# Attention's values made in four column tiles and turned by VectorE, with a fixed order for the attention's entrance and end

## The chip, the cores and the metric

One core of one Trainium2 chip runs the whole program. The metric is the device time of one execution in microseconds (us); lower is better. TensorE (PE in the profile) multiplies matrices and writes into PSUM; ScalarE (ACT) and VectorE (DVE) take the results from there; GpSimd (POOL) does sums in SBUF and issues some transfers, SyncE (SP) issues the others.

## The reference

Sixteen images of 256 channels, 28 x 28 pixels, pass four layers: a convolution with binary weights (layer 0), a block of binary convolutions with gates (layer 1), two binary convolutions with batch normalisation and a residual (layer 2), and an attention over the 784 pixels of each image (layer 3). Only the last is touched:

```python
def _L3_conv_ref(x, Wq, Wk, Wv, Wp):       # x: 16 x 256 x 28 x 28, float32
    C_RED = 64
    xf = x.reshape(B, C, N)                            # N = 784
    q = jnp.einsum('rc,bcn->bnr', Wq, xf)
    k = jnp.einsum('rc,bcn->brn', Wk, xf)
    v = jnp.einsum('rc,bcn->bnr', Wv, xf)
    attn = jnp.einsum('bnr,brm->bnm', q, k) * (1.0 / sqrt(64))
    attn = jax.nn.softmax(attn, axis=-1)
    out = jnp.einsum('bnm,bmr->brn', attn, v)
    out = jnp.einsum('cr,brn->bcn', Wp, out)
    return out.reshape(B, C, H, W) + x
```

The end of layer 2 is done at the start of the attention, image by image: `prelu(y * scale + shift + x, a3)`.

## The kernel before

An image lies in SBUF as x[b], 128 partitions x 2 channel halves x 784 pixels. The attention works on it transposed: the scores are laid out with 112 keys on the partitions (7 chunks of keys, c) and the 784 queries in two halves (h) of 392 along the free axis. The exponential is taken without subtracting a maximum; `watch` looks for overflow, and a second program part (not entered here) would redo the attention if it found one. Each image has these steps, and the loop weaves three images together:

- finish_a, finish_b, finish_c: the end of layer 2 for image b + 3 or b + 2 (normalise, relu, combine). From image 3 on the residual is added by a transfer that accumulates (`p<-x2d`); finish_c also stores the image for the second part (`xd`).
- queries_keys and project_v: queries, keys and values of the next image. PSUM tile `mi` holds queries on partitions 0 to 63 and keys on 64 to 127. The pool `ps_mi` has one buffer, and the projection at the end of an image uses it too.
- scores, exponentials `es`, sums of them for the softmax's denominator, values: 7 chunks each.
- denominators, reciprocal, normalisation, projection with Wp and the sum with x, store.

All operands are float32, for which the hardware does each matmul of the source in two passes; the profile counts both. `manual_schedule` keeps the instructions of each engine in the order of the source; outside of it the order is chosen by a scheduler. In the profile, L1084 is finish_a, L1094 finish_b (`rl`), L1099 finish_c, L1112 the queries' and keys' matmul (`mi`), L1116, L1118 and L1119 its copies, L1127 the scores (`sc`), L1131 the exponential, L1148 values (`av`) and denominators (`sm`), L1188 and L1192 the values' matmul and copy (`va`), L1198 the projection. x[b] is named `p` there.

```python
    pssc = ctx.enter_context(tc.tile_pool(name="ps_sc", bufs=2, space=PSUM))
    psav = ctx.enter_context(tc.tile_pool(name="ps_av", bufs=1, space=PSUM))
    psmi = ctx.enter_context(tc.tile_pool(name="ps_mi", bufs=1, space=PSUM))
    pssm = ctx.enter_context(tc.tile_pool(name="ps_sm", bufs=1, space=PSUM))
    ones = ph.tile([MC, 64], F32, name="ones64")
    nc.gpsimd.memset(ones, 1.0)
    # ... (na3, one_bank; two_banks gives a tile of two PSUM banks)

    def finish_a(b, n=slice(0, N)):
        for k in range(2):
            v = x[b][:, k, n]
            A.activation(v, v, AF.Identity, bias=bg3[:, k:k + 1], scale=sg3[:, k:k + 1])
            if b < 3:
                V.tensor_tensor(v, v, x2[b][:, k, n], ALU.add)
        if b >= 3:
            nc.gpsimd.dma_start(out=x[b], in_=x2d[b], accum_op=ALU.add)

    def finish_b(b, n=slice(0, N)):
        for k in range(2):
            if n.start == 0:
                rls[k] = buf(f"rl{k}", 1, shape=(P, N))
            A.activation(rls[k][:, n], x[b][:, k, n], AF.Relu, scale=-1.0)

    def finish_c(b, n=slice(0, N)):
        for k in range(2):
            v = x[b][:, k, n]
            V.scalar_tensor_tensor(v, rls[k][:, n], na3[:, k:k + 1], v, ALU.mult, ALU.add)
        if n.stop == N:
            nc.sync.dma_start(out=xd[b], in_=x[b])

    def queries_keys(b):
        ps = two_banks(psmi, "mi")
        q, k_ = qs[b], ks[b] = buf("q", 2, shape=(P, HN)), buf("k", 2)
        for h in range(2):
            for k in range(2):
                T.matmul(
                    ps[:, h, :HN], lhsT=wqk[:, k, :], rhs=x[b][:, k, h * HN:(h + 1) * HN],
                    start=(k == 0), stop=(k == 1),
                )
        A.copy(k_[64:P], ps[64:P, :, :HN])
        for h in range(2):
            A.copy(q[64 * h:64 * h + 64], ps[0:64, h, :HN])
        V.tensor_copy(k_[0:64], ps[64:P, :, :HN])

    # ... scores(b, c): for h in range(2) a matmul of 64 rows, lhsT = 112 keys of k_, rhs = q,
    # into the two banks of "sc"; then A.activation(es, sc, AF.Exp, scale=0.125)
    # ... sum_up: sums of es, chunks 0 to 3 on GpSimd, 4 to 6 on VectorE; sum_all adds the two
    # side_by_side: two matmuls, h = 0 and 1, into partitions 0 to 63 and 64 to 127
    # ... values: side_by_side(avs[b], va[b % 2][:, c, 0:64], es[b, c], ...) into PSUM "av"
    # take_values: ScalarE copies av to o; denominators: side_by_side(dns[b], ones, sums, ...)
    # invert: V.reciprocal(r, dns); normalize: V.tensor_tensor(o, o, r, mult)
    # watch: two ScalarE passes over dns and r with accum_out, which look for overflow

    def project_v(b):
        ps = one_bank(pssm, "sm")
        for c in range(NC_):
            for k in range(2):
                T.matmul(
                    ps[:MC, c * 64:(c + 1) * 64], lhsT=x[b][:, k, c * MC:(c + 1) * MC], rhs=wv[:, k, :],
                    start=(k == 0), stop=(k == 1),
                )
        A.copy(va[b % 2][:, :, 0:64], ps[:MC, :NC_ * 64].rearrange("p (c r) -> p c r", r=64))

    # ... project(b, mo): two matmuls, lhsT = wp, rhs = o, into a tile "mi" of psmi (or the one
    # given); then V.tensor_tensor adds it to x[b][:, mo]
    # ... store: nc.sync.dma_start(out=out[b], in_=x[b])

    for b in range(3):
        load_x2(b)
    for h in range(2):
        for step in (finish_a, finish_b, finish_c):
            step(0, slice(h * HN, h * HN + HN))
    queries_keys(0)
    scores(0, 0)
    project_v(0)
    for step in (finish_a, finish_b, finish_c):
        step(1)
    finish_a(2)

    with tc.manual_schedule(engines={ET.PE, ET.Activation, ET.DVE, ET.Pool}):
        for b in range(B):
            last = b == B - 1
            scores(b, 1)
            if b > 0:
                take_values(b - 1)
            if b > 1:
                project(b - 2, 0)
            sum_up(b, 1)
            scores(b, 2)
            if b > 0:
                sum_up(b - 1, 6)
            scores(b, 3)
            sum_up(b, 2, 3)
            if b > 1:
                watch(b - 2)
            finish_b(b + 2)                  # if b + 2 < B, as finish_c
            queries_keys(b + 1)              # if not last, as project_v
            project_v(b + 1)
            sum_all(b - 1)
            finish_c(b + 2)
            scores(b, 4)
            scores(b, 5)
            if b > 1:
                project(b - 2, 1)
                store(b - 2)
            sum_up(b, 5)
            if b + 3 < B:
                finish_a(b + 3)
            for c in range(4):
                values(b, c)
            if b > 0 and not last:
                denominators(b - 1)
                invert(b - 1)
            scores(b, 6)
            # ... (if not last:)
            scores(b + 1, 0)
            for c in range(4, NC_):
                values(b, c)
            normalize(b - 1)
            # ... (if last: denominators, reciprocal, projection and store of b - 1 among these)
        b = B - 1
        denominators(b)
        pss = [two_banks(pssc, "sc") for mo in range(2)]
        # ... in two parts n of 196 queries: take_values for both; then for each invert,
        # normalize, watch, project(b, mo, pss[mo], n) for mo = 0, 1; then store(b, mo) for both
```

Ahead of the attention 45 unused matmuls (`keep_busy`) hold TensorE active while the last statistics of layer 2 are worked out.

## Time and profile before

| | |
|---|---|
| time, median of 3 runs | 1153.67 us (1153.47 to 1154.21) |
| span of the profiled execution | 1151.9 us |
| mean granted TensorE clock | 0.991 |
| TensorE busy (matmul) | 1113.7 us, 97% |
| TensorE weight loads | 948.5 us, 82% |
| VectorE busy | 801.2 us, 70% |
| ScalarE busy | 711.5 us, 62% |
| GpSimd busy | 135.8 us, 12% |
| attention | from 849.3 (first mi) to 1151.9 us |

A line of the groups reads: source line, engine, operation, out<-in by the program's names with the tile of TensorE (rows*columns), shapes out<-in as partitions x elements, type, count; then busy time in us, mean ns of one instruction, and the engine's idle time just before such instructions with what ended it. Matmuls overlap in TensorE's pipeline, so their mean length is not what one adds to a sequence. The chain is followed backward from the last instruction: at each step to what released it, or to the instruction before it on its engine. The timeline merges neighbouring instructions of one kind into one row, with its start and busy time.

### The profile page before, as it was taken

What the parts mean: (1) busy time and instruction counts of PE and PEld (TensorE: products, weight loads), DVE (VectorE), ACT (ScalarE), POOL (GpSimd) and SP (SyncE); (2) the same over time, 40 slices, a digit from 0 to 9 for tenths busy, and PEclk for the clock granted to TensorE, in tenths of its full rate; (3) what the DMA queues carried; (4) which work ended last, traced back from release to release, by engine and by line L of the source; (5) the groups of instructions that cost most, each with busy time, mean ns of one, the idle gap of its engine ahead of it and who ended that gap; (6) DMA issues with size and microseconds to landing.
All of it is one profiled execution on the core that took longest, in us unless ns stands there. A gap on an engine that the chain in (4) does not pass through costs nothing.

```text
span 1151.9 us, 15800 instructions
## 1 busy us (share of the span) xinstructions
PE 1113.7 (97%) x6062; PEld 948.5 (82%) x6067; DVE 801.2 (70%) x1430; ACT 711.5 (62%) x1051; POOL 135.8 (12%) x134
## 2 busy tenths in 40 slices
PE   6998999999999999998999999999999999999995
PEld 6998989999999999994999998999955555555542
DVE  3775359899999999967576665566574667666565
ACT  4654445677777777765555554555576766767742
POOL 2000000000000000000000000000013443443421
PEclk9999999999999999999999999999999999999998
DMA  7553341222222231010680000000014355464422
GB/s 301 187 178 140 126 143 40 71 98 85 91 106 84 74 124 70 29 53 34 249 317 5 1 1 1 1 1 1 1 57 112 95 158 147 106 168 122 131 84 87
DMA packets 25973, 111.63 MB, mean 97 GB/s; under 512 B 3554, under 2 KB 6308, under 8 KB 25892
## 3 DMA queue, kind: packets, MB, share of 16 engines
q1 hardware_dynamic: 20436, 80.85, 20.0%
q0 software_dynamic: 5456, 29.71, 8.8%
q8 instruction: 50, 0.82, 0.3%
q14 instruction: 31, 0.25, 0.1%
HBM read 65.59 MB, written 44.96 MB: 96 GB/s over the span
## 4 chain that ended last, share of the span: by engine, by line
PE 79%; issue 5%; DVE 4%; ACT 2%; POOL 0%; POOLq 0%; ACTq 0%; DVEq 0%
PE cv L248 24%; PE cv L574 23%; PE sc L1127 7%; PE av L1148 7%; PE mi L1112 4%; PE sm L1188 4%; PE cv L678 3%; PE cv L267 2%; PE mi L1198 2%; PE unused L342 1%; PE sm L1148 1%; ACT fpads L933 1%; DVE r L1173 0%; PE hid L506 0%; PE gate L649 0%
## 5 line engine op out<-in xcount | busy, mean ns | idle before, releaser
L248 PE MATMUL cv<-fpads,wpk 128*128 128x392 f32 x1440 | 297.9, 360 | 11.3 <-DVE wpk L208 8.9
L574 PE MATMUL cv<-vs,w 128*128 128x392 f32 x1536 | 301.4, 354 | 0.0
L574 PEld LDWEIGHTS cv<-vs,w 128*128 128x128 f32 x1536 | 287.4, 190 | 1.6 <-issue 0.3
L248 PEld LDWEIGHTS cv<-fpads,wpk 128*128 128x128 f32 x1440 | 274.8, 194 | 15.7 <-issue 8.5
L963 DVE SCALAR_TENSOR_TENSOR p<-r,r,cv 128x392 f32<-128x392 f32 x128 | 78.6, 614 | 79.5 <-ACT r L960 79.5
L1131 ACT ACTIVATE es<-sc 112x784 f32<-112x784 f32 x112 | 87.2, 822 | 73.8 <-PE sc L1127 73.6
L248 PE MATMUL cv<-fpads,wpl 128*128 128x392 f32 x576 | 124.8, 352 | 0.0
L259 ACT ACTIVATE t<-cv,rounding 128x392 f32<-128x392 f32 x96 | 56.2, 586 | 88.0 <-PE cv L248 85.7
L248 PEld LDWEIGHTS cv<-fpads,wpl 128*128 128x128 f32 x576 | 108.9, 190 | 0.6
L1127 PE MATMUL sc<-q,k 64*112 64x392 f32 x448 | 89.0, 510 | 2.6 <-DVE k L1119 1.6
L960 ACT ACTIVATE r<-cv 128x784 f32<-128x784 f32 (+1 forms) x66 | 52.9, 805 | 60.0 <-PE cv L267 59.5
L260 DVE TENSOR_SCALAR uv<-t 128x392 fp32r<-128x392 f32 x96 | 35.0, 364 | 68.1 <-ACT t L259 68.1
L1148 PE MATMUL av<-es,va 112*64 112x392 f32 x448 | 80.8, 499 | 0.0
L1127 PEld LDWEIGHTS sc<-q,k 64*112 64x112 f32 x448 | 35.8, 172 | 43.3 <-issue 18.3
L1141 POOL TENSOR_TENSOR sum<-sum,es 112x784 f32<-112x784 f32 x32 | 68.5, 2139 | 2.5
L1148 PEld LDWEIGHTS av<-es,va 112*64 112x64 f32 x448 | 29.6, 136 | 47.4 <-issue 44.6
L103 DVE TENSOR_TENSOR vs<-pad 128x840 fp32r<-128x840 bf16 (+1 forms) x66 | 64.5, 1002 | 0.1
L481 ACT CAST n<-cv 128x784 int16<-128x784 f32 x32 | 26.0, 812 | 58.8 <-DVE l_parts L480 16.4
L1119 DVE COPY k<-mi 64x784 f32<-64x784 f32 x16 | 15.6, 976 | 64.2 <-ACT q L1118 64.2
L716 POOL DMA_DIRECT2D x2d<-x x16 | 8.5, 533 | 366.8 <-DVE x L710 304.0
L1202 DVE TENSOR_TENSOR p<-mi,p 128x784 f32<-128x784 f32 x30 | 29.2, 975 | 31.5 <-PE mi L1198 31.1
L1188 PEld LDWEIGHTS sm<-wv,p 128*112 128x112 f32 x448 | 46.7, 178 | 5.0 <-issue 2.6
(248 smaller groups left out, 1702.7 us busy)
## 6 DMA issues: line engine op xcount, KB each, us to landing
xs<-in_x_dram SPq DMA_DIRECT2D x32, 784.0 KB, 4.4
x2d<-x POOLq DMA_DIRECT2D x16, 784.0 KB, 3.6
xd<-p SPq DMA_DIRECT2D x16, 784.0 KB, 3.3
out_dram<-p SPq DMA_DIRECT2D x15, 784.0 KB, 5.3
p<-x2d SPq DMA_DIRECT2D x13, 784.0 KB, 9.0
p<-x2d POOLq DMA_DIRECT2D x13, 784.0 KB, 9.1
n0d<-n POOLq DMA_DIRECT2D x16, 392.0 KB, 2.7
n<-n0d SPq DMA_DIRECT2D x16, 392.0 KB, 3.1
```

The costliest lines, as they stand in the source:

```text
L103: V.tensor_tensor(o, a, b, op)
L248: T.matmul(pss[j][:, mo, :HN].rearrange("p (a b) -> p a b", b=S), lhsT=lhsT, rhs=pads[:, j // 2 % 2, k, r:r + HR, c:c + S], start=start, s ...
L259: A.activation(r, pss[j][:, 0, :HN], AF.Identity, bias=rounding, scale=1.0 / PACK)
L574: T.matmul(ps.rearrange("p (a b) -> p a b", b=S), lhsT=w[:, k, c, u, mo * P:(mo + 1) * P], rhs=vs[:, b % 2, u, k, :, c:c + S], start=(n == 0),
L960: A.activation(r[:, mo], ps[:, mo, :HN], AF.Relu, scale=-1.0)
L963: V.scalar_tensor_tensor(p, r[:, mo], beta[:, mo:mo + 1], ps[:, mo, :HN], ALU.mult, ALU.add)
L1112: T.matmul(ps[:, h, :HN], lhsT=wqk[:, k, :], rhs=x[b][:, k, h * HN:(h + 1) * HN], start=(k == 0), stop=(k == 1),)
L1127: T.matmul(ps[:MC, h, :HN], lhsT=k_[rows, c * MC:(c + 1) * MC], rhs=qs[b][rows], start=True, stop=True)
L1131: A.activation(e, ps[:MC, :, :HN], AF.Exp, scale=0.125)
L1141: (V if late else nc.gpsimd).tensor_tensor(sums[b, late], sums[b, late], e, ALU.add)
L1148: T.matmul(ps[64 * h:64 * h + 64, :HN], lhsT=w, rhs=e[:, h, :], start=start, stop=stop)
L1188: T.matmul(ps[:MC, c * 64:(c + 1) * 64], lhsT=x[b][:, k, c * MC:(c + 1) * MC], rhs=wv[:, k, :], start=(k == 0), stop=(k == 1),)
```

## The change

The values. Before, a chunk of 112 pixels of x was the stationary operand (128 x 112) and Wv (64 columns) moved, which gives values with the keys on the partitions, as the later matmuls need them: 14 matmuls per image in the source. Now 32 columns of Wv are stationary and a quarter of the image, 196 pixels, moves; four such column tiles work side by side, each on its quarter, and write partitions 32g to 32g + 31. That gives 16 matmuls in the source, with the pixels along the free axis. ScalarE copies them into `vt`, padded to blocks of 32, and VectorE turns each 32 x 32 block (`turn_v`), which puts the keys on the partitions. A chunk of keys is now made of 28 pixels of each of the four quarters, padded to 128 with zeros: the keys are stored as 7 x 4 x 32, the `ones` of the denominators have zeros in the padded rows, and the chunks of scores, exponentials and sums have 128 partitions for 112.

The keys are copied in halves: for each half h, ScalarE copies keys and queries, then VectorE the keys to the other partitions.

The entrance and the end. The steps of images 0 and 1 ahead of the loop are now in a fixed order as well, with image 0 in halves, and finish_a(2) is in the loop's first pass. The last image has its own order: the denominators, reciprocals and projections of images 14 and 15 are moved among its last values, and the sums of image 14 with x are separate from their projections.

The purpose is to have fewer and shorter matmuls on TensorE for the values and fewer pauses at the two ends. The diff, cut to its core (left out are constants and signatures, the tiles of the padded keys, `ones` and va with their memsets, the argument ks of finish_a, and empty lines):

```diff
@@ -1101,41 +1115,46 @@
             nc.sync.dma_start(out=xd[b], in_=x[b])
     rls = [None, None]
-    qs, ks = [None] * B, [None] * B
...   (removed: queries_keys, as above)
+    qs = [None] * B
+    def queries_keys(b, h, ps):
+        for k in range(2):
+            T.matmul(
+                ps[:, h, :HN], lhsT=wqk[:, k, :], rhs=x[b][:, k, h * HN:(h + 1) * HN], start=(k == 0), stop=(k == 1)
+            )
+    def queries(b, h, ps):
+        if h == 0:
+            qs[b] = buf("q", 2, shape=(P, HN))
+        A.copy(qs[b][64 * h:64 * h + 64], ps[0:64, h, :HN])
+    def keys_to(b, rows, h, ps):
+        copy = A.copy if rows else V.tensor_copy
+        copy(
+            keys[b % 2][64 * rows:64 * rows + 64, :, 2 * h:2 * h + 2, 0:GC].rearrange("p c g i -> p g c i"),
+            ps[64:P, h, :HN].rearrange("p (g c i) -> p g c i", g=2, i=GC),
+        )
     es, sums = {}, {}
     def scores(b, c):
-        ps, k_ = two_banks(pssc, "sc"), ks[b].rearrange("p h n -> p (h n)")
+        ps = two_banks(pssc, "sc")
+        chunk = keys[b % 2].rearrange("p c g i -> p c (g i)")[:, c, :]
         for h in range(2):
             rows = slice(64 * h, 64 * h + 64)
             T.matmul(
-                ps[:MC, h, :HN], lhsT=k_[rows, c * MC:(c + 1) * MC], rhs=qs[b][rows], start=True, stop=True
+                ps[:, h, :HN], lhsT=chunk[rows], rhs=qs[b][rows], start=True, stop=True
             )
-        e = es[b, c] = buf("es", 7, shape=(MC, 2, HN))
-        A.activation(e, ps[:MC, :, :HN], AF.Exp, scale=0.125)
+        e = es[b, c] = buf("es", 7)
+        A.activation(e, ps[:, :, :HN], AF.Exp, scale=0.125)
...   (sum_up)
-                sums[b, late] = buf(f"sum{c}", 2, shape=(MC, 2, HN))
+                sums[b, late] = buf(f"sum{c}", 2)
@@ -1163,11 +1182,12 @@
         A.copy(os[b][0][:, n], avs[b][:, n])
     def denominators(b):
-        dns[b] = one_bank(pssm, "sm")
+        dns[b] = two_banks(pssc, "sc")[:, 0, :] if b == B - 1 else one_bank(pssm, "sm")
         parts = [sums[b, False], sums[b, True], es[b, NC_ - 1]] if b == B - 1 else [sums[b, True]]
         for i, e in enumerate(parts):
-            side_by_side(dns[b], ones, e, i == 0, i == len(parts) - 1)
+            side_by_side(dns[b], ones.rearrange("p a i -> p (a i)"), e, i == 0, i == len(parts) - 1)
     def invert(b, n=slice(0, HN)):
         V.reciprocal(os[b][1][:, n], dns[b][:, n])
@@ -1183,42 +1203,65 @@
     def project_v(b):
         ps = one_bank(pssm, "sm")
...   (removed: the body of project_v, as above)
+        for a in range(2):
+            for k in range(2):
+                for g in range(4):
+                    T.matmul(
+                        ps[32 * g:32 * g + 32, a * GN:(a + 1) * GN], lhsT=wv[:, k, 32 * a:32 * a + 32],
+                        rhs=x[b][:, k, g * GN:(g + 1) * GN], start=(k == 0), stop=(k == 1),
+                    )
+        A.copy(
+            vt[:, :, :, 0:GC].rearrange("p c a i -> p a c i"),
+            ps[:, 0:2 * GN].rearrange("p (a c i) -> p a c i", a=2, i=GC),
+        )
+    def turn_v(b):
+        V.transpose(va[b % 2].rearrange("p c r -> p (c r)"), vt.rearrange("p c a i -> p (c a i)"))
+    projected = {}
+    def project(b, mo, ps=None, n=slice(0, HN), add=True):
+        ps = projected[b, mo] = ps or two_banks(psmi, "mi")
         for h in range(2):
             rows = slice(64 * h, 64 * h + 64)
...
+        if add:
+            add_up(b, mo, n)
+    def add_up(b, mo, n=slice(0, HN)):
         v = halves(x[b][:, mo, :])[:, :, n]
-        V.tensor_tensor(v, ps[:, :, n], v, ALU.add)
+        V.tensor_tensor(v, projected[b, mo][:, :, n], v, ALU.add)
     def store(b, mo=slice(0, 2)):
         nc.sync.dma_start(out=out[b][:, mo], in_=x[b][:, mo])
     for b in range(3):
         load_x2(b)
-    for h in range(2):
-        for step in (finish_a, finish_b, finish_c):
-            step(0, slice(h * HN, h * HN + HN))
-    queries_keys(0)
-    scores(0, 0)
-    project_v(0)
-    for step in (finish_a, finish_b, finish_c):
-        step(1)
-    finish_a(2)
     with tc.manual_schedule(engines={ET.PE, ET.Activation, ET.DVE, ET.Pool}):
-        for b in range(B):
-            last = b == B - 1
+        parts = [slice(h * HN, h * HN + HN) for h in range(2)]
+        ps = two_banks(psmi, "mi")
+        for h in range(2):
+            for step in (finish_a, finish_b, finish_c):
+                step(0, parts[h])
+            queries_keys(0, h, ps)
+            if h == 0:
+                keys_to(0, 1, 0, ps)
+                queries(0, 0, ps)
+                keys_to(0, 0, 0, ps)
+        finish_a(1, ks=(0,))
+        keys_to(0, 1, 1, ps)
+        queries(0, 1, ps)
+        keys_to(0, 0, 1, ps)
+        scores(0, 0)
+        finish_a(1, ks=(1,))
+        project_v(0)
+        turn_v(0)
+        finish_b(1)
+        finish_c(1)
+        for b in range(B - 1):
             scores(b, 1)
             if b > 0:
                 take_values(b - 1)
@@ -1230,17 +1273,23 @@
                 sum_up(b - 1, 6)
             scores(b, 3)
             sum_up(b, 2, 3)
+            if b == 0:
+                finish_a(2)
             if b > 1:
                 watch(b - 2)
             if b + 2 < B:
                 finish_b(b + 2)
-            if last:
+            ps = two_banks(psmi, "mi")
+            for h in range(2):
+                queries_keys(b + 1, h, ps)
+            for h in range(2):
+                keys_to(b + 1, 1, h, ps)
+                queries(b + 1, h, ps)
+                keys_to(b + 1, 0, h, ps)
+            project_v(b + 1)
+            if b > 0:
                 sum_all(b - 1)
-            else:
-                queries_keys(b + 1)
-                project_v(b + 1)
-                if b > 0:
-                    sum_all(b - 1)
+            turn_v(b + 1)
             if b + 2 < B:
                 finish_c(b + 2)
             scores(b, 4)
@@ -1251,33 +1300,52 @@
             sum_up(b, 5)
             if b + 3 < B:
                 finish_a(b + 3)
-            if last:
-                denominators(b - 1)
-                invert(b - 1)
-                normalize(b - 1)
-                watch(b - 1)
             for c in range(4):
                 values(b, c)
-            if b > 0 and not last:
+            if b > 0:
                 denominators(b - 1)
                 invert(b - 1)
             scores(b, 6)
-            if last:
-                project(b - 1, 0)
-            else:
-                scores(b + 1, 0)
+            scores(b + 1, 0)
             for c in range(4, NC_):
                 values(b, c)
-            if last:
-                project(b - 1, 1)
-                store(b - 1)
-            else:
-                if b > 0:
-                    normalize(b - 1)
+            if b > 0:
+                normalize(b - 1)
         b = B - 1
+        scores(b, 1)
+        take_values(b - 1)
+        project(b - 2, 0)
+        sum_up(b, 1)
+        scores(b, 2)
+        sum_up(b - 1, 6)
+        scores(b, 3)
+        sum_up(b, 2, 3)
+        watch(b - 2)
+        sum_all(b - 1)
+        scores(b, 4)
+        scores(b, 5)
+        project(b - 2, 1)
+        store(b - 2)
+        for c in range(2):
+            values(b, c)
+        denominators(b - 1)
+        invert(b - 1)
+        sum_up(b, 5)
+        normalize(b - 1)
+        for c in range(2, 4):
+            values(b, c)
+        scores(b, 6)
+        watch(b - 1)
+        for c in range(4, 6):
+            values(b, c)
         denominators(b)
-        pss = [two_banks(pssc, "sc") for mo in range(2)]
+        project(b - 1, 0, add=False)
+        sc = two_banks(pssc, "sc")
+        project(b - 1, 1, sc, add=False)
+        values(b, 6)
+        pss = [two_banks(psmi, "mi"), sc]
         parts = [slice(0, HN // 2), slice(HN // 2, HN)]
         for n in parts:
             take_values(b, n)
@@ -1285,6 +1353,10 @@
             invert(b, n)
             normalize(b, n)
             watch(b, n)
+            if n.start == 0:
+                for mo in range(2):
+                    add_up(b - 1, mo)
+                store(b - 1)
             for mo in range(2):
                 project(b, mo, pss[mo], n)
         for mo in range(2):
```

## The prediction

> **What bounds the kernel now.** I read the chain that ended last first, to learn which engine sets the end.
>
> ```profile
> PE 79%; issue 5%; DVE 4%; ACT 2%; POOL 0%; POOLq 0%; ACTq 0%; DVEq 0%
> ```
>
> TensorE sets it. The change touches only the attention, from about 849 us to the end at 1151.9. Next, the groups by shape in that stretch, for what one instruction costs (after the bar: busy us, mean ns, idle time before it and its releaser):
>
> ```profile
> L1188 PE MATMUL sm<-wv,p 128*112 128x64 f32 x448 | 46.1, 260 | 0.0
> L1112 PE MATMUL mi<-p,wqk 128*128 128x392 f32 x128 | 46.6, 506 | 0.1
> L1119 DVE COPY k<-mi 64x784 f32<-64x784 f32 x16 | 15.6, 976 | 64.2 <-ACT q L1118 64.2
> L1118 ACT COPY q<-mi 64x392 f32<-64x392 f32 x32 | 15.3, 479 | 0.4
> L1192 ACT COPY va<-sm 112x448 f32<-112x448 f32 x16 | 8.5, 532 | 4.5 <-PE sm L1188 4.4
> ```
>
> The first row is what the change attacks: 448 matmuls for the values, 28 per image (the source's 14, each in two fp32 passes). Its 260 ns is one's latency. The chain in one steady image gives what the group takes (start, us, what):
>
> ```profile
> 1086.84 2.83 PE mi L1112 x8
> 1089.67 2.71 PE sm L1188 x28
> 1092.38 1.50 PE sc L1127 x8
> 1093.88 0.66 PE mi L1198 x4
> 1094.54 2.78 PE av L1148 x16
> ```
>
> Values: 2.71 us for 28, or 0.097 each. The av rows give a second price: 16 matmuls of 392 columns in pairs of column tiles, 2.78/8 = 0.35 per pair (0.329 from pair to pair in single instructions, where the second of a pair starts 6.5 ns after the first). So two small tiles cost what one does. TensorE has no pause here: from one mi to the next, 1086.8 to 1104.4, are 17.6 us, and the stretch shows it busy for 17.60.
>
> Now who stands close behind it. The timeline of the same image (start, busy, engine, in brackets the idle time before):
>
> ```profile
> 1088.87 1.59 ACT L1094 ACTIVATE rl<-p 128x784 f32<-128x784 f32 x2
> 1090.47 0.81 ACT L1116 COPY k<-mi 64x784 f32<-64x784 f32 x1
> 1091.29 0.97 ACT L1118 COPY q<-mi 64x392 f32<-64x392 f32 x2
> 1092.29 0.98 DVE L1119 COPY k<-mi 64x784 f32<-64x784 f32 x1 [3.78 <-ACT q L1118]
> 1093.72 0.82 PE L1198 MATMUL mi<-o,wp 64*128 64x392 f32 x4
> ```
>
> With M the start of mi (1086.8), ScalarE is held by the two rl until M+3.7, then copies; VectorE's copy of the keys waits for the queries' copy and ends at M+6.5. The projection L1198 writes the same PSUM tile, which has one buffer, so it cannot start before that; TensorE comes to it at M+6.95. The slack is only 0.45 us. That decides my number.
>
> Last, the entrance and the clock at the end (of the stretch line: length, then busy us of PE, PEld, DVE, ACT, POOL, then the granted clock):
>
> ```profile
> 849.29 2.24 PE L1112 MATMUL mi<-p,wqk 128*128 128x392 f32 x6
> 856.47 1.57 PE L1127 MATMUL sc<-q,k 64*112 64x392 f32 x8 [1.55 <-DVE k L1119]
> 859.98 2.90 PE L1112 MATMUL mi<-p,wqk 128*128 128x392 f32 x8
> ```
>
> ```profile
> 1138.00:1152.00 14.00, 2.89 (x20) 1.87 (x18) 6.09 (x11) 1.77 (x8) 0.00 (x0) 0.64 0.28 112
> ```
>
> [...]pairs start 6.5 ns apart, and the first pair after a change takes 0.38 to 0.43 us instead of 0.329. No four-column tiling occurs in this trace. [...]There is no transpose of this size before; I give it the rate of the copies. [...]0.64 in the last 14 us, where TensorE is mostly idle.
>
> **The change part by part.**
>
> *Values on TensorE.* Eight groups of four 32-column tiles, 196 columns each, 32 matmuls. If four run side by side as two do, a group costs 196/392 of 0.329, 0.165 us; 8 x 0.165 = 1.32, plus about 0.1 for one more change of form (mi to values). 2.71 - 1.42 = 1.3 us less per image, 20 us over 16 if all lay on the path.
>
> *The new VectorE work.* From copies of 784 columns at 0.975 us and of 392 at 0.567, the slope is 1.04 ns per column plus 0.16 fixed. The turn of 448 columns: about 0.6 us per image, not on TensorE's path if the values come late enough (they are read from M+7.7 on).
>
> *The keys, which now are copied by half.* In the program ScalarE copies keys 0 and queries 0, then VectorE keys 0; only after that ScalarE may take keys 1 and queries 1, then VectorE keys 1, and the projection waits for this last copy. With ScalarE's copies of 392 columns at 0.485 from start to start, VectorE's at 0.57, and hand-overs of 0.03 and 0.05: 0.97 + 0.03 + 0.57 + 0.05 + 0.97 + 0.03 + 0.57 = 3.19 us. Before it was 0.81 + 0.97 + 0.03 + 0.98 = 2.79. It still starts at M+3.7, as the rl ahead of it are unchanged, so it ends at M+6.9, and with 0.08 of hand-over the projection starts at M+7.0. TensorE, 1.3 us quicker with the values, is there at M+5.7. It waits 1.3 us. **The steady image therefore keeps its 17.6 us, or takes 17.7**: the saving becomes a wait for VectorE. For the 12 full images: 12 x 0.1 = +1.2.
>
> *VectorE's load.* Two copies of 0.57 for one of 0.98, and the turn: +0.75 us beside a busy 11.7 of 17.6. It works without a break from the keys to the normalisation, which ended at M+14.48; now at about M+15.4, against its reader on TensorE at M+15.5. Just enough.
>
> *Chunks of 128 keys for 112, padded.* They lengthen partitions, not columns: scores, exponentials, sums and values cost the same.
>
> *The entrance.* ScalarE is now in a fixed order: it finishes half 0, waits for mi of half 0, copies its keys and queries, and only then goes on with half 1. TensorE is held by 45 filler matmuls until 849.24, so mi of half 0 cannot end before 850.8, and ScalarE idles from 848.3 to there. Following each engine: half 1 is finished near 855, keys 1 by 857, first scores at 857.6 (856.47 before). Image 1's last finishing steps now come behind the values' copy, so its mi starts near 864.0 (859.98 before); image 2's near 879.2 (876.25); image 3's at 896.8 (893.19). From there on the steady rhythm holds: **+3.6 us**.
>
> *The end.* In the cycle of image 14 there is no rl ahead of the copies, so the chain of keys ends about 1 us sooner and some 0.7 of the TensorE saving comes through. In the last image the sums' matmuls (the denominators) move ahead of the last values, so VectorE's wait for them (1.15 us at 1138.1) and the first reciprocal (1.38) go beside TensorE work: -2.5. Together -3.2. The tail from the last sum to the end (1145.8 to 1151.9, the store) is the same.
>
> *Sum.* 1153.7 + 3.6 + 1.2 - 3.2 = 1155.3; I say 1155.
>
> **The rivals.**
>
> *The whole saving arrives.* If VectorE could copy keys 0 while ScalarE copies keys 1, the chain would end near M+6.0 and TensorE would gain about 1.25 us in 15 images: -19, with the end 1132. For it: TensorE is the chain's 79%, and has no pause. Against: the waits run in a strict alternation, and the slack was 0.45 us, so at most that much of 1.3 could come through without shortening the chain.
>
> *A transfer takes the path.* Each image's reload and its store are issued within about half a us of each other, and a reload takes this long:
>
> ```profile
> p<-x2d POOLq DMA_DIRECT2D x13, 784.0 KB, 9.1
> ```
>
> The rl waited for it hardly at all (0.3 us in 13). Issued near M+10.2, it lands at M+19.3; the next rl wants it at 17.6 + 2.1 = M+19.7. With the turn ahead of it, VectorE releases it about 0.9 us later: M+20.2, a period of 18.1, and 13 images cost 6 us: 1161. [...]Which of them the new order puts first, this trace does not tell.
>
> *Four tiles do not overlap.* Then 32 x 0.165 = 5.3 us per image, 2.6 more than before, and no slack hides it: 15 x 2.5 = +37, about 1191. Against: pairs overlap almost fully, and the tiles write different partitions.
>
> *A cold clock at the entrance.* TensorE pauses from about 850.7 to 854.4[...]; mi and scores after it would take up to 2 us more: 1157.
>
> **Range and chances.** The low end takes about two thirds of the first rival, since my chain rests on waits read from the program and could be looser on the chip; the high end takes transfer, clock and some of both: 1142 to 1164. A gain of over 2% needs -23 us, more than the first rival gives: 0.04. A loss of over 2% needs +23, which only unoverlapped tiles give: 0.03. Within: 0.93.
>
> **What would show it.** Values: 32 matmuls in 1.3 to 1.45 us; 5 would be the third rival. Steady image: TensorE idle for 1.0 to 1.3 us before the projection, put down to VectorE's copy of keys, and 17.6 to 17.7 us from mi to mi. If that wait is missing and the period is near 16.4, I am wrong by the first rival; 18 or more with rl waiting for the reload is the second. Entrance: first scores at 857.6, mi of image 3 near 896.8. End: the last sum about 3 us earlier, measured from mi of image 14. The weakest steps are the entrance, followed by hand over four engines, and whether each half's copies really alternate.

## The result, and the profile after

The changed kernel takes 1170.81 us (median of 4 runs, 1169.17 to 1174.65) and the kernel before 1153.57 (4 runs, 1152.39 to 1154.21): a ratio of 1.0155, 95% interval 1.0129 to 1.0181. It is 17 us slower. The prediction was 1155, with 1164 as its upper end.

The start of each mi group (the eight matmuls for queries and keys, one group per image) divides the two profiles into the three stretches of the prediction's sum:

| stretch | before | after | change | predicted |
|---|---|---|---|---|
| first mi to the fourth (entrance) | 43.8 | 51.2 | +7.4 | +3.6 |
| fourth to the sixteenth (12 steady images) | 211.2 | 225.7 | +14.5 | +1.2 |
| sixteenth mi to the end | 47.6 | 44.7 | -2.9 | -3.2 |
| sum | 302.6 | 321.6 | +19.0 | +1.6 |

The two profiled spans differ by 17.1 us and not by 19.0, because the first mi starts at 849.3 us in the profile before and at 847.4 in the one after. What lies ahead of it is unchanged code, and its start varies between 847 and 850 from profile to profile.

The chain that ended last, first line of the profile after:

```profile
PE 66%; issue 7%; ACT 5%; DMA 5%; DVE 4%; POOL 2%; POOLq 0%; ACTq 0%; DVEq 0%
```

Of the chain TensorE had 79% before and has 66% now; ScalarE grew from 2 to 5% and a transfer appears with 5%, where there was none. The groups by shape in the attention (after the bar: busy us, mean ns, idle time before and its releaser):

```profile
L1227 PE MATMUL mi<-o,wp 64*128 64x392 f32 x116 | 26.5, 530 | 21.9 <-DVE keyswa L1134 21.2 <-DVE o L1197 0.7
L1209 PE MATMUL sm<-p,wv 128*32 128x196 f32 x512 | 24.5, 332 | 0.0
L1108 ACT ACTIVATE rl<-p 128x784 f32<-128x784 f32 x30 | 24.2, 850 | 10.5 <-DMA p<-x2d 7.2 <-DVE p L1100 3.3
L1134 DVE COPY keyswa<-mi 64x392 f32<-64x392 f32 x32 | 18.2, 568 | 75.9 <-ACT q L1130 75.9
L1219 DVE STREAM_TRANSPOSE v<-vt 128x448 f32<-128x448 f32 x16 | 10.1, 633 | 0.0
```

The second row is the new values' matmul, 24.5 us busy where the old one had 46.1. So what the change was made for has happened. The first row shows where it went: TensorE now sits idle for 21.2 us ahead of the projection until VectorE's copy of the keys. The third row shows that ScalarE's rl waits 7.2 us for the reload, for which it waited 0.3 before. One image of the changed kernel in the chain (start, us, what), from the landing of a reload to the values:

```profile
964.19 10.71 DMA p<-x2d
...
974.93 1.61 ACT rl L1108 x2
...
976.55 0.48 ACT keyswa L1134
...
977.04 0.49 ACT q L1130
...
977.55 0.58 DVE keyswa L1134
...
978.16 0.48 ACT keyswa L1134
...
978.65 0.48 ACT q L1130
...
979.16 0.58 DVE keyswa L1134
...
979.87 1.31 PE mi L1227 x4
981.18 4.05 PE av L1167 x16
```

Before, this window of the chain held TensorE alone. Now an image begins with a transfer, goes through rl and through the six alternating copies (3.2 us from 976.55 to 979.74), and only then comes to TensorE. The last row has a second peculiarity: these 16 matmuls took 2.78 us in the kernel before and take 4.05 here. Three neighbouring images (start and end; length; busy us of PE, PEld, DVE, ACT and POOL, each with its number of instructions; granted clock, DMA share, GB/s) show why:

```profile
953.20:971.62 18.42, 16.67 (x111) 7.67 (x109) 12.32 (x13) 12.69 (x22) 7.04 (x5) 1.00 0.47 131
971.62:992.29 20.67, 18.30 (x110) 8.02 (x108) 12.42 (x13) 12.68 (x22) 7.05 (x5) 0.92 0.50 140
992.29:1010.09 17.80, 16.67 (x111) 7.67 (x109) 12.32 (x13) 12.58 (x22) 7.04 (x5) 1.00 0.40 113
```

The clock was halved for 3.4 us of the middle one, after TensorE's pause of 2.4 us. The steady images of the changed kernel are uneven, 17.8 to 21.0 us, where those before were 17.60 each, but for one of 17.67; and behind the three long images come one of 18.1 and two of 17.8, the least there is.

The transfers of the changed kernel (KB each, median us from issue to landing):

```profile
out_dram<-p SPq DMA_DIRECT2D x15, 784.0 KB, 9.5
p<-x2d POOLq DMA_DIRECT2D x13, 784.0 KB, 10.3
```

They were 5.3 and 9.1. The theory formed from this, which the experiments test: there is a **ring** of waits. rl of an image waits for its reload; rl holds the copies of keys and queries up; the steps behind them end in the issue of the next reload; and the rl of the next image waits for that one. From rl to the issue of the reload it took 8.1 us before and takes 8.3 now, and with the reload 17.2 before (less than TensorE's 17.60) and 18.2 to 19.3 now. Rivals: the alternating copies alone, wherever they start; VectorE full; the halved clock.

### The profile page after: what moved, and what is told of

The parts are those of the page before. It is cut to its first block, busy times and chain, and to the rows that moved or that the text cites. A ratio compares the mean times of both kernels' runs of the same rounds, so it can differ in the third digit from the quotient of the medians.

```text
span 1169.0 us, 15992 instructions
## 1 busy us (share of the span) xinstructions
PE 1105.6 (95%) x6131; PEld 919.3 (79%) x6131; DVE 813.0 (70%) x1463; ACT 712.7 (61%) x1067; POOL 138.7 (12%) x138
## 4 chain that ended last, share of the span: by engine, by line
PE 66%; issue 7%; ACT 5%; DMA 5%; DVE 4%; POOL 2%; POOLq 0%; ACTq 0%; DVEq 0%
PE cv L575 24%; PE cv L249 24%; DMA p<-x2d 5%; PE av L1167 4%; PE cv L679 3%; PE sc L1146 2%; PE cv L268 2%; PE unused L343 1%; POOL sum L1160 1%; PE mi L1227 1%; ACT rl L1108 1%; DVE keyswa L1134 1%; ACT q L1130 1%; ACT keyswa L1134 1%; ACT es L1150 1%
## 5 line engine op out<-in xcount | busy, mean ns | idle before, releaser
L1150 ACT ACTIVATE es<-sc 128x784 f32<-128x784 f32 x112 | 87.4, 825 | 79.0 <-PE sc L1146 79.0
L1146 PE MATMUL sc<-q,keyswa 64*128 64x392 f32 x448 | 90.8, 517 | 6.9 <-ACT es L1150 5.2
L1167 PE MATMUL av<-es,v 128*64 128x392 f32 x448 | 86.1, 524 | 0.0
L1146 PEld LDWEIGHTS sc<-q,keyswa 64*128 64x128 f32 x448 | 39.0, 187 | 50.2 <-issue 23.8
L1167 PEld LDWEIGHTS av<-es,v 128*64 128x64 f32 x448 | 30.8, 143 | 52.5 <-issue 49.8
L1134 DVE COPY keyswa<-mi 64x392 f32<-64x392 f32 x32 | 18.2, 568 | 75.9 <-ACT q L1130 75.9
L1160 POOL TENSOR_TENSOR sum<-sum,es 128x784 f32<-128x784 f32 x32 | 68.7, 2148 | 2.9 <-ACT es L1150 0.5
L1227 PE MATMUL mi<-o,wp 64*128 64x392 f32 (+1 forms) x124 | 28.1, 528 | 25.9 <-DVE keyswa L1134 21.2
L1123 PE MATMUL mi<-p,wqk 128*128 128x392 f32 x128 | 46.7, 506 | 3.6 <-DVE p L1113 3.5
## 6 DMA issues: line engine op xcount, KB each, us to landing
p<-x2d POOLq DMA_DIRECT2D x13, 784.0 KB, 10.3
```

The source lines that it names most:

```text
L1123: T.matmul(ps[:, h, :HN], lhsT=wqk[:, k, :], rhs=x[b][:, k, h * HN:(h + 1) * HN], start=(k == 0), stop=(k == 1))
L1134: copy(keys[b % 2][64 * rows:64 * rows + 64, :, 2 * h:2 * h + 2, 0:GC].rearrange("p c g i -> p g c i"), ps[64:P, h, :HN].rearrange("p (g c ...
L1146: T.matmul(ps[:, h, :HN], lhsT=chunk[rows], rhs=qs[b][rows], start=True, stop=True)
L1150: A.activation(e, ps[:, :, :HN], AF.Exp, scale=0.125)
L1160: (V if late else nc.gpsimd).tensor_tensor(sums[b, late], sums[b, late], e, ALU.add)
L1167: T.matmul(ps[64 * h:64 * h + 64, :HN], lhsT=w, rhs=e[:, h, :], start=start, stop=stop)
```

## The experiments

**rl behind the copies.** On ScalarE the order of two steps is exchanged:

```diff
-            finish_b(b + 2)
             ps = two_banks(psmi, "mi")
             ...   (queries_keys, keys_to, queries)
+            finish_b(b + 2)
             project_v(b + 1)
```

> The changed kernel with one step moved on ScalarE: the two rl of image b+2 come behind the copies of keys and queries instead of ahead of them. Reload theory (a ring rl, keys and queries, finishing, reload transfer, next rl takes 18.3 us and sets the image): the ring is opened, because rl no longer holds the keys up; the copies begin at mi's end (M+2.7) and end near M+5.9, TensorE reaches the projection at M+5.7, so its wait falls from 1.1-2.7 us to about 0.3, and the steady image takes 16.6 to 16.9 us for 18.8 on average: about 1145 us. Keys theory (the alternation of the two engines' copies alone is the bound, 3.2 us long wherever it starts): the same direction, but the alternation still ends 0.2 us after TensorE, so no telling apart by this run alone. Rival (VectorE with its added turn is full, and the normalisation comes too late for the next projection): the wait moves to that projection, image about 17.5 us, 1156.

Measured: 1152.78 us (12 runs; ratio to the kernel before 1.0006, 0.9997 to 1.0014), 18 us less than the changed kernel. All steady images take 17.29 us, none of them waits for its reload, the clock stays full. TensorE's wait before the projection was 21.2 us in total and is now, from the view of waits (us in total, times, longest):

```profile
PE mi L1227 <- DVE keyswa L1134: 4.9, 13, 0.4
```

The ring is open, but 17.29 is 0.4 to 0.7 more than the 16.6 to 16.9 expected. The projection behind the copies starts at 6.26 us after mi, as VectorE's last copy ends at 6.11 and TensorE could have been there at 5.7; and the image's other projection starts at 15.11, 0.05 after the normalisation ends (15.06). So the rival about VectorE was half right.

**Reload one image earlier.**

```diff
-            if b + 3 < B:
-                finish_a(b + 3)
+            if b == 0:
+                finish_a(3)
+            if b + 4 < B:
+                finish_a(b + 4)
```

> The changed kernel with ScalarE's normalisation, and with it the reload transfer, of each image done one image earlier (b+4 in the pass of b, image 3 as well in the first pass); keys and all else as they are. Reload theory: no rl waits for a transfer any more (7.2 us in 10 waits before), every steady image takes what images 8 and 13 take now, 17.8 us with 1.1 us of TensorE wait, and the clock stays full[...]: 12 x (18.8 - 17.8) = -12, about 1159 us (up to 2 more from the extra work in the first pass). Keys theory: the transfer's wait is only a by-product, time stays at 1169 to 1172.

Measured: 1161.66 us (ratio 1.0070, 1.0053 to 1.0087). Every image from the fourth to the fifteenth takes 17.80 us, with the clock full, and rl no longer waits for its reload:

```profile
ACT rl L1108 <- DMA p<-x2d: 0.6, 1, 0.6
```

The copies were left as they were, so the ring and not the alternation makes the 18.8. It also gives the size of the alternation by itself: 17.80 against 17.60, 0.2 us an image, or 2.3 us in 12. The remaining 12.2 of the 14.5 go with the ring: in the changed kernel the waits of rl add 7.2 us, and three images with a halved clock 1.65 each. Moving rl gains a further 6.1 us (213.6 to 207.5 in the twelve images), as the copies then also start earlier. (That the time is 1161.7 and not 1159 lies mainly in the entrance, which took 53.1 us in this profile.)

**The halves of mi in PSUM tiles of their own.** Each half of queries and keys gets a tile of one bank, so that VectorE's copy of one half need not wait for ScalarE's copies of the other, nor they for it:

```diff
-            ps = two_banks(psmi, "mi")
+            ps = [one_bank(psmi, f"mi{h}") for h in range(2)]
...   (the same in project; add_up in two halves)
```

> The changed kernel with the two halves of mi as two PSUM tiles of one bank each, so that VectorE copies keys of half 0 while ScalarE is at half 1; the sum with x becomes two instructions of half the size (VectorE +0.2 us each). The chain of copies falls from 3.17 to about 2.54 us. Keys theory: the image falls by what the chain falls and TensorE's wait with it, to 17.2 us: 12 x 1.6 = -19, about 1152. Reload theory: the ring is 0.65 us shorter, 18.3 to about 17.7, the long pauses and with them the halved clocks go: about 1158 us, with rl still waiting for its reload in some images.

Measured: 1161.83 us (ratio 1.0067, 1.0045 to 1.0090). The copies take 2.56 us instead of 3.17. Still rl waits for its reload, 11.1 us in 11 images, the images take 17.1 to 20.6 us, and two of them show the halved clock. The shorter chain of copies shortened the ring by about that much and no more (from rl to the issue of the reload 7.7 us instead of 8.3); the keys theory's 1152 is out.

**The turn late.** `turn_v(b + 1)` moves from ahead of `finish_c(b + 2)` to behind `normalize(b - 1)`, at the end of the pass.

> The changed kernel with VectorE's turn of the values moved from ahead of the finishing step to behind the normalisation at the end of the pass (its result is read one pass later). If VectorE's added work is what lengthens the ring, all of its 0.65 us leaves: 12 x 0.65 = -8, about 1163 us. Reload theory in its exact form: the reload waits for ScalarE's normalisation too, which ends only 0.1 us before VectorE's step, so the reload is issued at most 0.1 us sooner; what may come is that the store xd, 0.65 us sooner, is out of the reload's way: 1164 to 1170 us. Keys theory: no change, 1170.

Measured: 1164.28 us (ratio 1.0098, 1.0081 to 1.0114). Eight of the twelve steady images take 17.8 us, and the reload takes 9.4 us. The reload is issued no sooner after rl than before (8.3 us), as the exact form of the theory had it; what improved is the transfer itself.

**The store xd left out.** The store of the finished image for the second program part, which is not entered, is left out for images 3 to 15. This kernel lacks what that part would need.

> The changed kernel without the stores xd of images 3 to 15 (the finished image, kept for the second program part, which is not entered; left out to take one transfer out of the ring's way). Ring theory: the reload and the result's store have the queues to themselves, the reload lands in 9 us or less, the ring is below 17.7 and all images take 17.8: about 1158 us. Rival (the reload's time is its own): no change, 1170.

Measured: 1160.85 us (ratio 1.0067, 1.0046 to 1.0087). The view of waits on ScalarE, and then the transfer:

```profile
ACT rl L1108 <- DMA p<-x2d: 1.1, 1, 1.1
```

```profile
p<-x2d POOLq DMA_DIRECT2D x13, 784.0 KB, 8.1
```

The reload is issued at the same moment as in the changed kernel and lands 2.2 us sooner; all steady images but one take 17.80. So the 2.2 us that the reload had more are due to the store xd. That it matters how close ahead xd is issued is what the runs together suggest (medians of the eleven reloads issued in steady images; the kernels not listed fit to about 0.2 us):

| kernel | xd issued ahead of the reload by, us | result's store issued behind it by, us | reload, median, us |
|---|---|---|---|
| changed | 0.17 | 0.83 | 10.3 |
| turn late | 0.69 | 0.31 | 9.4 |
| before | 0.89 | 0.11 | 9.15 |
| rl behind the copies | 1.02 | -0.02 | 9.0 |
| three edits (below) | 1.62 | -0.55 | 8.6 |
| no xd | none | 0.83 | 8.1 |

**The result's store one pass later.** It was meant to send the store out straight behind xd.

> The changed kernel with the store of each image's result issued one pass later, straight behind the store xd, so that it goes out within 0.3 us of the reload as in the kernel before, and not 0.84 us behind it. Ring theory with the transfer's time as its open term: the reload takes 9.1 to 9.5 us as in the kernel before (10.4 in the changed one), the ring falls from 18.7 to 17.7, no rl waits, all images 17.8 us: about 1158 us. Rival ([...]the reload is slow because of VectorE's and ScalarE's later work): still 10 us and more, 1168 to 1171.

Measured: 1174.03 us (ratio 1.0179, 1.0154 to 1.0204). The store was still issued 0.83 us behind the reload, so the condition that was to be tested did not arise, and the run says nothing of the store's part. The view of waits puts the issue down to VectorE's sum with x in the same pass (L1235), as in the changed kernel, although that sum belongs to another image. Why it waits for that one is not known.

**Fillers in the pause.** Two unused matmuls in TensorE's pause, ahead of the projection that waits for the keys, are meant to keep TensorE active and the clock full.

> The changed kernel with two unused matmuls (four in hardware, 1.3 us) on TensorE ahead of the second projection, in its pause, writing where the next values will be written over. Nothing else is shortened. Clock theory (the images of 20 to 21 us are those in which a pause of about 2 us or more halved the clock for 3.4 us, 1.65 us each): no image above 19 us, clock 1.00 in all steady images, 5 us less and some 1 to 2 us for the fillers' own time: about 1167 us. Rival (the long images are long by the transfers, and the clock follows): unchanged, images above 20 us stay.

Measured: 1172.56 us (ratio 1.0170, 1.0152 to 1.0187), no gain. The clock was full in all steady images, and yet the twelve take 226.5 us as against 225.7. The wait went back to where the ring has it:

```profile
ACT rl L1108 <- DMA p<-x2d: 12.3, 12, 2.9
```

In the changed kernel this was 7.2. An image with the halved clock had TensorE busy there for 18.30 to 18.35 us where the others had 16.67, about 1.65 more, and meanwhile the next reload landed; with the clock full rl waited for most of that time. So the clock theory falls as the main cause. The halving is not quite free: in the changed kernel the rl behind the three long images came 0.5, 1.0 and 0.7 us after their reloads had landed, which gives an estimate of 2.2 us for what the halved clock costs on top of the ring. The run with fillers does not show this gain, as its reloads took 2.7 us more in the twelve images, one of them 12.5 us; why is not known.

**Entrance.** Image 2's first finishing step is put back ahead of the loop; and, in another kernel, the whole entrance of the kernel before is put in.

> The changed kernel with image 2's first finishing step (ScalarE's normalisation and VectorE's two sums) back ahead of the loop, behind image 1's finishing, instead of inside the first pass. In the changed kernel those two sums take 2.5 us each instead of 0.98 while GpSimd adds exponentials, and the rl, the keys' copies and the projection queue behind them. Theory (the collision with GpSimd costs the first pass its 3 us): the second to third mi takes 16.5 us instead of 19.9, no halved clock there, about 1167 us. Rival (the 2 us of ScalarE only move ahead and delay the first scores and mi of image 1 by as much): the first pass loses 3, the entrance before it gains 2 to 3, 1170 us.

> The changed kernel with the entrance of the kernel before: image 0 is finished in both halves before its mi, order left to the scheduler, image 1 and the first step of image 2 ahead of the loop; the new copies by half and the turn stay. Theory: the third mi comes 27 us after the first, as before, instead of 34.5: -7, about 1164 us, with the steady images unchanged at 18 to 19 us on average. Rival (the entrance only shifts where the transfers' ring is waited for): the gain is under 2 us.

Measured: 1170.03 us for the first (ratio 1.0151, 1.0134 to 1.0168) and 1165.52 for the second (1.0121, 1.0103 to 1.0139). In the first, second to third mi takes 16.7 us instead of 19.9, as expected; but the second mi comes 18.7 us after the first instead of 14.6, with the clock at 0.80 up to 858 us and 0.88 to 866, so nothing is gained: the rival. (Some of these 4 us are the clock's: in six other profiles with the new entrance and a clock of 0.79 or 0.80 between these two mi, the second comes after 16.5 to 16.9 us.) With the old entrance the fourth mi comes 43.6 us after the first (51.2 changed, 43.8 before), the clock is full, and the time is 5.3 us less than the changed kernel's. What the new entrance costs, the timeline of the changed kernel shows:

```profile
852.46 1.58 PE L1123 MATMUL mi<-p,wqk 128*128 128x392 f32 x4 [3.50 <-DVE p L1113]
...
863.69 4.39 POOL L1160 TENSOR_TENSOR sum<-sum,es 128x784 f32<-128x784 f32 x2
863.87 5.05 DVE L1100 TENSOR_TENSOR p<-p,x 128x784 f32<-128x784 f32 x2 [1.99 <-ACT p L1098]
...
866.41 0.86 ACT L1108 ACTIVATE rl<-p 128x784 f32<-128x784 f32 x1 [1.64 <-DVE p L1100]
```

Two costs: TensorE pauses 3.5 us between the halves of image 0's mi (in eight of ten profiles with the new entrance the granted clock was 0.73 to 0.90 from 846 to 858 us, in two, the changed kernel's among them, 1.00); and VectorE's two sums of image 2, moved into the first pass, take 5.05 us instead of 2 x 0.98, while GpSimd is adding exponentials. VectorE's sums, begun 0.18 us after GpSimd's, took 2.5 and 2.6 us each here, and 0.97 in the kernel before, where GpSimd is idle at that time (0.00 us busy from 846 to 858).

**The old end.** The kernel before's last image, in the changed kernel.

> The changed kernel with the end of the kernel before (last image's order, denominators in their own PSUM tile). The prediction gave the new end -3.2 us, of which 0.7 belong to the pass of image 14 and 2.5 to the reordered last image. If that holds, from mi of image 15 to the end takes 47.3 us instead of 44.7, and the time is 2.5 us more, about 1173 us; if the end is only a rearrangement of waits, no change.

Measured: 1176.10 us (ratio 1.0201, 1.0184 to 1.0218). From the sixteenth mi to the end it takes 47.2 us, 44.7 with the new end: the new end is worth 2.5 us. The profile, which is 3 us above the median, also has 2 us more in the entrance (with a halved clock) and 2 in the uneven steady images than the changed kernel's.

**Three edits together**, rl behind the copies, tiles of their own, the turn late; then with two of them, and with the old entrance added; and the first edit alone in the kernel before, as a control.

> Three of the edits before together in the changed kernel: rl behind the copies of keys and queries, the halves of mi in PSUM tiles of their own, the turn behind the normalisation. Theory: each removes one wait on TensorE's path (rl ahead of the copies; VectorE's last copy; the normalisation, which in the first of these runs came 0.05 us before its reader). The copies begin at M+2.2 and end at M+4.8, TensorE comes to the projection at M+5.7 and waits for nothing; the image takes 17.6 less what the values gave up, 1.25: 16.35 to 16.5 us, with the entrance as it is now: 1153 + 7 - 3 - 12 x 1.2 = about 1143 us. Rival (VectorE full: 12.6 us busy of 16.4, with the sums split in two): the normalisation holds the image at 17.0 or more, 1150 us or more.

> Two of the three edits, without the PSUM tiles of their own: shows what the alternation of the two engines' copies costs once rl and the turn are out of the way. The copies end at M+6.1, TensorE comes at M+5.7 and needs a restart of about 0.2: image 17.0 us, 12 x 0.3 less than with rl moved alone: about 1149 us. Rival (the alternation costs nothing once it starts early): 16.4 to 16.6 us, 1143.

> The three edits (rl behind the copies, halves of mi in tiles of their own, turn late) and the entrance of the kernel before in place of the new fixed one. Steady image 16.39 us as with the three; the fourth mi after the first comes 41 to 43 us, for 47.9 with the three alone: -5 to -6, about 1134 us. Rival (the scheduler's order is made worse by the copies by half): 1138 to 1140.

> Control: the kernel before, with only rl moved behind the copies of keys and queries. There TensorE has no pause in the steady image, so a theory in which the gain of this order comes only from what the values gave up says: nothing, 17.60 us per image, 1151.5 to 1153 us. Rival (the order helps by itself): 1148 us or less.

| kernel | time, us | ratio to before, 95% interval | steady image, us |
|---|---|---|---|
| before (medians of its runs beside these) | 1151.9 to 1153.6 | | 17.60 |
| changed | 1170.81 | 1.0155 (1.0129 to 1.0181) | 18.81 on average |
| control: before, rl behind the copies | 1152.62 | 1.0000 (0.9991 to 1.0008) | 17.60 |
| changed, rl behind the copies | 1152.78 | 1.0006 (0.9997 to 1.0014) | 17.29 |
| and the turn late | 1148.89 | 0.9967 (0.9953 to 0.9981) | 17.04 |
| and the tiles of their own | 1139.39 | 0.9892 (0.9870 to 0.9913) | 16.39 |
| and the old entrance | 1132.55 | 0.9821 (0.9805 to 0.9838) | 16.39 |

The last three rows each add an edit to the row above. The steady images of these four runs came out as expected (17.60; 17.04 for 17.0; 16.39 for 16.35 to 16.5; 16.39), and the last kernel's fourth mi comes 41.9 us after its first, as expected. Of the 0.90 us by which 17.29 exceeds 16.39, the turn's place takes 0.25 and the shared PSUM tile 0.65. The last kernel is the fastest of this study, 20 us below the one before. One steady image of it in the chain, and the copies in its timeline:

```profile
1053.52 2.83 PE mi L1126 x8
1056.35 1.46 PE sm L1212 x32
1057.81 1.52 PE sc L1149 x8
1059.33 0.66 PE mi L1230 x4
1059.99 2.78 PE av L1170 x16
```

```profile
1055.66 0.48 ACT L1137 COPY keyswa<-mi 64x392 f32<-64x392 f32 x1
...
1056.65 0.48 ACT L1137 COPY keyswa<-mi 64x392 f32<-64x392 f32 x1
1056.66 0.57 DVE L1137 COPY keyswa<-mi 64x392 f32<-64x392 f32 x1 [1.46 <-ACT q L1133]
...
1057.65 1.61 ACT L1108 ACTIVATE rl<-p 128x784 f32<-128x784 f32 x2
1057.65 0.57 DVE L1137 COPY keyswa<-mi 64x392 f32<-64x392 f32 x1 [0.42 <-ACT q L1133]
...
1059.16 0.82 PE L1230 MATMUL mi<-o,wp 64*128 64x392 f32 x4
```

The chain is TensorE alone again, and the values' group has become 1.46 us where it was 2.71: those 1.25 us, and hardly anything else, are the 17.60 - 16.39. In the timeline ScalarE's second copy of keys and VectorE's first start together, rl comes behind them, and the last copy ends at 1058.2, 0.9 us before the projection wants it. The control says that moving rl is worth nothing by itself: in the kernel before TensorE had no pause to give. The other edits were not tried there.

## Why the prediction was wrong

*Values on TensorE: right.* 1.42 us was worked out for 32 matmuls with the change of form, 1.46 measured. Four column tiles run side by side as two do: the four matmuls of a group start within 0.02 us, and the groups start 0.165 us apart (0.19 behind the first). They are 32 where there were 28, so not fewer, but four at a time.

*The turn: right.* 0.6 us worked out, 0.633 measured.

*The keys by half: right as a mechanism and nearly in size.* 3.19 us worked out, 3.17 measured; the projection at 7.0 us after mi, 7.01 measured in the images that wait for no transfer; the image 17.7 there, 17.80 measured. The strict alternation was disputed by the first rival; giving the two halves their own PSUM tiles let the copies run side by side. ScalarE's copies of the queries read partitions 0 to 63 and VectorE's copies of the keys 64 to 127, and yet VectorE's waits ended with the queries' copies (75.9 us in 32 waits). With the two tiles the copies took 2.56 us for 3.17; why the tile decides is not shown.

*The step that failed: that the steady image therefore takes 17.6 or 17.7, the reload costing nothing.* It put the transfer among the rivals, at 18.1 us an image and 1161 in all, and left it out of the sum. The ring is closed and takes 18.2 to 19.3, and the images took 18.81 on average. The rival had the mechanism and mis-sized its two terms: it moved the reload's issue 0.9 us later at an unchanged 9.1 us. The runs show the opposite: from rl, the issue is only 0.2 us later (8.3 for 8.1), and the reload takes 10.3. VectorE's added work moves the store xd, which it releases, but hardly the reload, which was released by ScalarE before; so the two came within 0.17 us of each other. Nor did the order of issue against the result's store make the reload quick: the reload was issued 0.83 us ahead of it, for 0.11 before, and was slower.

*VectorE's load, "just enough": right while the keys came late* (normalisation ends at 15.18, its reader starts at 15.72, in the images that wait for no transfer), and a bound of 0.25 us an image as soon as they came early, in the run with rl moved.

*Chunks of 128 keys for 112: right.* An exponential takes 0.825 us for 0.822, a sum on GpSimd 2.148 for 2.139; in the last kernel's chain eight matmuls of scores take 1.52 for 1.50 and sixteen of values 2.78 as before.

*The entrance: half right, and 3.8 us of the miss.* The second mi was put 4.0 us later relative to the kernel before, 3.9 measured. But the following pass was taken as 15.2 us and took 19.9: in it two sums of VectorE, which take 0.98 us undisturbed, ran beside GpSimd's and took 5.05.

*The end: right.* -3.2 predicted, -2.9 measured; of it 2.5 in the reordered last image, as predicted, and 0.3 for 0.7 in the pass of image 14.

*The cold clock rival* was foreseen for the entrance only, where it did appear in most of these profiles (0.73 to 0.90). In the steady images it appears too, where by the estimate above most of its time is time that rl would have waited anyway.

*The first rival*, that the whole saving arrives (1132), was not what this change does, but is reached with four edits: 1132.55. That the two numbers agree is partly luck: the rival's sum of -19 and the end leaves out the +3.6 of the entrance (with it, 1135), and the fourth edit takes the new entrance out again.

What stays open: how much of the reload's 10.3 us is due to the result's store issued close behind it. The distance to xd alone fits the table, but both distances change in it, and the run meant to part them did not.

## What to carry to other kernels

When a change shortens the engine that sets the end, look for every closed ring of waits that passes through other engines and a transfer, and add up its length around once: the ring that was 0.4 us shorter than the bound is the next bound, and what is added to it (1.4 us here, 1.2 of it in the transfer) comes back once per image. Do not carry a transfer's time over unchanged when an edit moves its issue or its neighbour's (here the same 784 KB took from 8.1 to 10.3 us): ask what it will then stand next to. And where a saving vanishes into a wait, first try the order of the instructions ahead of that wait: here two steps exchanged on ScalarE gave back 18 us, and it took three more edits to come 20 us below the kernel before.

## What the runs showed of the hardware that was not expected

- Some of TensorE's pauses of about 2 to 3 us were followed by a halved clock, and not by length alone: in the changed kernel's profile images with 1.96, 2.37 and 2.67 us of idle time were followed by 3.4 us of half clock, and one with 1.99 was not; with the result's store moved, 1.98 was and 2.87 was not. In the changed kernel the half clock began at 874.48, 980.29, 1038.32 and 1075.87 us and lasted 3.412 to 3.414 us each time, and these beginnings lie 31, 17 and 11 times 3.413 us apart. What decides which pause is followed by it is not shown.
- A reload of 784 KB took 8.1 us with the store xd left out and 10.3 with it, of the same size, issued 0.17 us ahead (the result's store 0.83 us behind in both).
- Two VectorE sums with both inputs in SBUF took 2.5 and 2.6 us beside GpSimd's sums, 0.97 without.
- VectorE's turn of 128 x 448 float32 in 32 x 32 blocks takes 0.633 us.
